# An attention layer's output projection: products per batch, or Strassen's seven products over pairs of batches

## The chip, the cores and the metric

One core of a Trainium2 chip runs the kernel. The time is device microseconds of one execution; the number given for a kernel is the median of its runs. Lower is better.

## What is computed

Multi-query attention with a residual, for 64 batches of 128 tokens, width 512, 16 heads of 64, one key and value head, all in float32:

```
xn = layernorm(x, g_in)
q = xn @ Wq                      # 512 -> 1024, 16 heads
k, v = xn @ Wkv                  # one head of 64 each, plus a null key and value
sim = q k^T + attn_bias          # causal and key mask set to a large negative
out = softmax(sim) @ v           # 128 x 1024 per batch
return x + layernorm(out @ Wo, g_out)     # Wo: 1024 -> 512
```

## The kernel before

The order of each engine's work is the program's order: a manual schedule, no reordering. `step(n)` runs for n = -6 to 62 and does one stage each for several batches: exponentials, block transpose and its DMAs for batch n+1, scores for n+2, values for n, output product and residual for n-1, and the input's norm, keys and query products some batches ahead. Tiles rotate in pools, so a write to a reused buffer waits for its last reader. [...]

- Query products (`product`, L408): groups of four batches; for each of four column parts f, seven products in Strassen's form with 256 output columns and two contraction chunks. `keep` (L419, ScalarE) copies an intermediate out of PSUM (kp1, ku2, ku3), `q_out` (L426 ScalarE, L429 VectorE) writes a quarter of qT, adding such a copy. Products 4 and 3 of part f come a step later. The token sums they need are GpSimd's (`token_sum`, L390), the weight sums VectorE's (`weight_sums`).
- Scores (`scores`, L474 and L485): first the upper 64 queries against all 128 keys, then the lower 64 against 64 keys. For each half VectorE adds the scores to the prepared bias rows S (L495) and takes the row maximum (L496). `bias_add` (L445) and `null_copy` on GpSimd prepare S; there are two S buffers.
- `exps` (L505): eight exponentials per half on ScalarE, then `rinv` (L522, VectorE) and `scale` (L526, GpSimd).
- `blocks_T` (L541): VectorE transposes S in 32x32 blocks into sb; `blocks_move` (L561) issues 14 DMAs on SP that carry the blocks to their places in aTb. One sb and one aTb buffer.
- `values` (L610): eight matmul calls into two `ps_w` banks (po), first with 64 rows, then with 128; ScalarE evacuates both into oT (L618).
- `out_mm` (L630): oT times Wo, eight chunks of 512 columns into one `ps_w` bank py. `out_stats` (L637 to L644): VectorE takes statistics of py and writes y = (py - mean) * g_out; GpSimd makes rstd. `residual`: ScalarE scales y by rstd (L658), GpSimd adds x (L659); `store` sends it.
- `norm_stats`/`norm_apply` (L231 to L249), `tokens_T` (L268), `k_T`/`kv_mm` into one bank pk (L298, L332) and their copies by VectorE (L310 to L337) prepare later batches.

In a float32 matmul call the profile shows two passes.

## Time and profile before

| | |
|---|---|
| median of 3 runs | 1196.62 us (1195.54 to 1200.66) |
| profiled execution | 1194.94 us; its span 1193.1 us |
| granted TensorE clock | 0.991 |
| output product L630 | 453.6 us busy in 1024 passes |
| query products L408 | 1680 passes of 256 columns |
| steady window 300 to 600 us | TensorE busy 300.0, VectorE 189.3, ScalarE 172.7, GpSimd 171.4 |

Busy time of overlapping instructions is counted once per engine; a row's mean is the time of one instruction from start to end, and pipelined instructions overlap by some of it. The last column of a row is the idle time just ahead of it on its engine, with what ended it.

### The profile page before, as it was taken

To read this page: it belongs to the slowest core of one execution; us is meant where nothing else is said; L and a number is where in the kernel's file an instruction comes from. 1 tells how busy PE (TensorE), PEld (TensorE's weight loads), DVE (VectorE), ACT (ScalarE), POOL (GpSimd) and SP (SyncE) were. 2 spreads that over 40 slices of the span, in tenths; PEclk is the share of its full clock that TensorE was granted. 3 is DMA by queue.
4 is the path that set the end of the run, shared out by engine and by line. 5 is a ranking of instruction groups with operands and counts; after the bars stand their busy time and mean duration, and the time that the engine had idled before them with its cause. 6 is when DMAs were issued, how large, how long until landed. Compare 5 with 4: busy or idle time off the path is not lost.

```text
span 1193.1 us, 22640 instructions
## 1 busy us (share of the span) xinstructions
PE 1151.9 (97%) x7588; PEld 747.9 (63%) x7588; DVE 716.2 (60%) x1449; ACT 652.1 (55%) x2625; POOL 654.4 (55%) x524
## 2 busy tenths in 40 slices
PE   6888999999999999999999999999999999999887
PEld 4465666666666666666666666666666666666433
DVE  6565566566666656656665665666566565545552
ACT  2254555565565556556555655655665565555551
POOL 5453755556475555647555465746546574654641
PEclk9998999999999999999999999999999999999999
DMA  6314334343533434343343434334353433422221
GB/s 185 111 39 127 96 124 122 119 122 90 143 95 122 121 112 130 90 136 103 122 115 116 131 91 133 105 123 111 111 140 90 130 99 106 102 74 71 70 81 45
DMA packets 107844, 129.79 MB, mean 109 GB/s; under 512 B 29264, under 2 KB 72528, under 8 KB 105936
## 3 DMA queue, kind: packets, MB, share of 16 engines
q1 hardware_dynamic: 106912, 127.29, 37.2%
q8 instruction: 61, 1.00, 0.4%
q10 hardware_dynamic: 816, 1.05, 0.2%
q14 instruction: 55, 0.45, 0.1%
HBM read 54.86 MB, written 31.46 MB: 72 GB/s over the span
## 4 chain that ended last, share of the span: by engine, by line
PE 86%; SPq 4%; DVE 2%; DMA 1%; issue 1%; ACT 0%; POOL 0%; DVEq 0%; ACTq 0%
PE py L630 35%; PE pa L408 17%; PE pc L408 8%; PE po L610 8%; PE ps L474 5%; PE pk L298 5%; PE pw L408 4%; SPq L561 4%; PE ps L485 3%; DMA aTb<-sb 1%; DVE sb L541 1%; PE pk L332 1%; DMA res<-in_x_dram 0%; DVE s L495 0%; PE paL L582 0%
## 5 line engine op out<-in xcount | busy, mean ns | idle before, releaser
L630 PE MATMUL py<-wo,oT 128*128 128x512 f32 x1024 | 453.6, 596 | 1.9 <-ACT oT L618 1.9
L445 POOL TENSOR_TENSOR s<-biasp,mneg 128x1536 f32<-128x1536 f32 x64 | 220.8, 3451 | 292.6 <-DVE sb L541 193.6
L505 ACT ACTIVATE s<-s,nmax 128x129 f32<-128x129 f32 (+1 forms) x1024 | 368.8, 365 | 0.0
L630 PEld LDWEIGHTS py<-wo,oT 128*128 128x128 f32 x1024 | 195.3, 191 | 223.9 <-issue 217.0
L526 POOL TENSOR_TENSOR s<-s,rinv 128x1024 f32<-128x1024 f32 (+1 forms) x128 | 188.4, 1479 | 15.5 <-DVE rinv L522 11.3
L505 ACT ACTIVATION_READ_ACCUMULATOR s<-s,nmax 128x1 f32 x1024 | 194.1, 190 | 0.0
L618 ACT ACTIVATE oT<-po,nv 128x512 f32<-128x512 f32 x128 | 81.3, 685 | 185.3 <-PE po L610 185.1
L495 DVE TENSOR_TENSOR s<-ps,s 128x1024 f32<-128x1024 f32 (+1 forms) x128 | 121.7, 951 | 68.9 <-PE ps L474 66.0
L659 POOL TENSOR_TENSOR y<-y,res 128x512 f32<-128x512 f32 x63 | 80.3, 1274 | 151.0 <-ACT y L658 151.0
L522 DVE RECIPROCAL rinv<-rsum 128x8 f32<-128x8 f32 x128 | 25.9, 203 | 209.7 <-ACT s L505 208.2
L408 PE MATMUL pa<-xS,wS 128*128 128x256 f32 x480 | 130.6, 395 | 0.7 <-ACT ku L419 0.7
L496 DVE TENSOR_REDUCE nmax<-s 128x8 f32<-128x1032 f32 (+1 forms) x128 | 123.1, 962 | 4.4
L610 PE MATMUL po<-aTb,vs 128*64 128x256 f32 (+1 forms) x768 | 109.8, 393 | 1.8 <-DVE aTb L589 1.7
L541 DVE STREAM_TRANSPOSE sb<-s 128x1536 f32<-128x1536 f32 x62 | 109.7, 1769 | 0.1
L419 ACT COPY ku<-pa 128x256 f32<-128x256 f32 x120 | 44.7, 373 | 116.1 <-PE pa L408 114.5
L408 PEld LDWEIGHTS pa<-xS,wS 128*128 128x128 f32 x480 | 83.0, 191 | 30.3 <-issue 20.0
L249 ACT ACTIVATE x<-x,nmr,rstd 128x512 f32<-128x512 f32 x60 | 48.7, 813 | 86.3 <-DVE nmr L248 85.9
L429 DVE TENSOR_TENSOR qT<-pw,kp 128x256 f32<-128x256 f32 x60 | 25.5, 425 | 98.5 <-ACT kp L419 98.5
L474 PEld LDWEIGHTS ps<-kT,qT 64*128 64x128 f32 x1024 | 62.5, 188 | 22.5 <-issue 21.8
L474 PE MATMUL ps<-kT,qT 64*128 64x128 f32 x1024 | 74.9, 286 | 0.0
L426 ACT COPY qT<-pa 128x256 f32<-128x256 f32 x60 | 22.4, 372 | 92.1 <-PE pa L408 92.1
L637 DVE BATCH_NORM_STATS2 sto<-py 128x6 f32<-128x512 f32 x64 | 44.8, 699 | 44.6 <-PE py L630 44.5
(90 smaller groups left out, 1547.4 us busy)
## 6 DMA issues: line engine op xcount, KB each, us to landing
aTb<-sb SPq DMA_DIRECT2D x372, 64.0 KB
x<-in_x_dram SPq DMA_DIRECT2D x64, 256.0 KB
res<-in_x_dram SPq DMA_DIRECT2D x64, 256.0 KB
out_dram<-y SPq DMA_DIRECT2D x64, 256.0 KB
aTb<-sb SPq DMA_DIRECT2D x496, 32.0 KB
xd<-xb SPq DMA_DIRECT2D x14, 1024.0 KB
xT<-xd SPq DMA_DIRECT2D x56, 256.0 KB
wo<-in_L_cond_Wo_dram SPq DMA_DIRECT2D x1, 2048.0 KB
```

Source lines behind the costliest of these rows:

```text
L408: nc.tensor.matmul(prod[tag], w[:, kc, f * P : (f + 1) * P], t[:, :, kc, :], start=(start and kc == 0), stop=(kc == HK - 1), skip_group_ch ...
L445: nc.gpsimd.tensor_tensor(S[b][:, :, 1 : ROW - 1], biasp, mneg[g][:, t].unsqueeze(1).broadcast_to([P, R8, NL + N]), ALU.add,)
L474: nc.tensor.matmul(pv[:, r, f, :], qT[g][rows, f, t, 1].rearrange("p u i -> p (u i)"), kT[b][rows, :], start=True, stop=True,)
L495: nc.vector.tensor_tensor(sv, pv, sv, ALU.add)
L496: nc.vector.tensor_reduce(nmax[b][:, hf], S[b][:, :, WITH_NULL[hf]], AX.X, ALU.max, negate=True)
L505: nc.scalar.activation(row, row, AF.Exp, bias=nmax[b][:, hf, k : k + 1], accum_out=rsum[b][:, hf, k : k + 1],)
L526: nc.gpsimd.tensor_tensor(sv, sv, rinvs.pop((b, hf)).unsqueeze(2).broadcast_to([P, R8, sv.shape[2]]), ALU.mult,)
L541: nc.vector.transpose(sb.rearrange("p j e q -> p e j q"), S[b][:, :, 1 : ROW - 1].rearrange("p e (j k) -> p e j k", k=Q),)
L610: nc.tensor.matmul(po[u][r * DH : (r + 1) * DH, half], vals, aTb[rows, slots, r * NF : (r + 1) * NF], start=True, stop=True,)
L618: nc.scalar.activation(oT[b][:, u * NF : (u + 1) * NF, :].rearrange("p f (s q) -> p s f q", q=Q), po[u].rearrange("p h i f q -> p (h i) f q"),
L630: nc.tensor.matmul(py, oT[b][:, c, :], wo[:, c, :], start=(c == 0), stop=(c == NC - 1))
L659: nc.gpsimd.tensor_tensor(y, y, res.pop(b), ALU.add)
```

## The change

Batches 1 to 60 are taken in 30 pairs (p, p+1), p odd; 0, 61, 62 and 63 stay as they were. A pair's two 128x1024 by 1024x512 products become seven products of half size, with 256 output columns and four contraction chunks each. GpSimd makes four sums of oT halves per pair, in place, and four sums of Wo halves once. Products 1 and 2 are issued in the even step n = p+1, products 5, 6, 7 and 3 in n = p+2, product 4 in n = p+3. Two new one-bank PSUM buffers X and Y (`ps_y`) hold the running sums; `ps_s` goes from two score buffers to one. `out_keep` and `out_part` move the results, and write y in SBUF in halves. `pair_norm` writes the normed rows into bank Y, `pair_residual` multiplies by g_out and adds x on VectorE. Both batches are stored together, and the residual is loaded one step later.

Also moved: lower scores before upper, each added as soon as it is there, the upper ones after the values; the block transpose right after the first add; the exponentials in parts between the other ScalarE work; `norm_apply` after them; query product 2 (in odd steps to the front); token sums 1 and 2 to the end of the step before; a weight sum to GpSimd, in place of its input.

```diff
-    ps_s = ctx.enter_context(tc.tile_pool(name="ps_s", bufs=2, space=PSUM))
+    ps_s = ctx.enter_context(tc.tile_pool(name="ps_s", bufs=1, space=PSUM))
     ps_q = ctx.enter_context(tc.tile_pool(name="ps_q", bufs=1, space=PSUM))
+    ps_y = ctx.enter_context(tc.tile_pool(name="ps_y", bufs=1, space=PSUM))
...
     def loads_late(n):
-        if 0 <= n:
+        if 1 <= n and not plain(n - 1):
+            load_res(n - 1)
+        if 0 <= n and plain(n):
             load_res(n)
...
-        nc.vector.tensor_tensor(s3, a11, a21, ALU.subtract)
...
+    def weight_sum_3():
+        nc.gpsimd.tensor_tensor(s3, a11, a21, ALU.subtract)
...
-    KEYS = UK, LK
-    WITH_NULL = slice(1 + NL, ROW), slice(0, 1 + NL)
+    KEYS = LK, UK
+    WITH_NULL = slice(0, 1 + NL), slice(1 + NL, ROW)
...
+    def scores_add(b, hf):
+        sv = S[b][:, :, KEYS[hf]].rearrange("p (r f) j -> p r f j", r=2)
+        nc.vector.tensor_tensor(sv, pss.pop((b, hf)), sv, ALU.add)
...
-    def exps(b, hf):
-        if hf == 0:
+    def exps(b, hf, lo=0, hi=R8):
+        if hf == 0 and lo == 0:
             rsum[b] = small.tile([P, 2, R8], FP, tag="rsum", name=f"rsum_{b}")
-        for k in range(R8):
+        for k in range(lo, hi):
             row = S[b][:, k, WITH_NULL[hf]]
...
+    def paired(p):
+        return 1 <= p <= P_LAST and p % 2 == 1
+    def plain(b):
+        return not (paired(b) or paired(b - 1))
+    def out_weight_sum(k):
+        p, m = ((e12, e11), (e22, wT[:, 0]), (e22, e12), (e21, wT[:, 1]))[k]
+        nc.gpsimd.tensor_tensor(wT[:, k], p, m, ALU.subtract)
+    def out_sums(p):
+        yS[p] = bp.tile([P, HC, N], FP, tag="yS", name=f"yS_{p}", bufs=1)
+        h11, h12 = oT[p][:, lo_c], oT[p][:, hi_c]
+        h21, h22 = oT[p + 1][:, lo_c], oT[p + 1][:, hi_c]
+        nc.gpsimd.tensor_tensor(yS[p], h21, h22, ALU.add)
+        nc.gpsimd.tensor_tensor(h21, h11, h21, ALU.subtract)
+        nc.gpsimd.tensor_tensor(h11, yS[p], h11, ALU.subtract)
+        nc.gpsimd.tensor_tensor(h12, h12, h11, ALU.subtract)
+    def out_product(p, k, pool, tag, start=True):
+        key = "y" + tag
+        if start:
+            prod[key] = pool.tile([P, HE], FP, tag=tag, name=f"py{tag}_{p}_{k}")
+        a, b = oT[p], oT[p + 1] if p + 1 in oT else None
+        h, w = {
+            1: lambda: (a[:, lo_c], e11),
+            2: lambda: (a[:, hi_c], e21),
+            3: lambda: (a[:, hi_c], e22),
+            4: lambda: (b[:, hi_c], wT[:, 3]),
+            5: lambda: (yS[p], wT[:, 0]),
+            6: lambda: (a[:, lo_c], wT[:, 1]),
+            7: lambda: (b[:, lo_c], wT[:, 2]),
+        }[k]()
+        for c in range(HC):
+            nc.tensor.matmul(
+                prod[key],
+                h[:, c, :],
+                w[:, c, :],
+                start=(start and c == 0),
+                stop=(c == HC - 1),
+                skip_group_check=not start,
+            )
+    def out_keep(tag, name, slot):
+        kept[name] = bp.tile([P, HE], FP, tag=f"k{slot}", name=f"k{name}", bufs=1)
+        if name == "yu2":
+            nc.vector.tensor_copy(kept[name], prod["y" + tag])
+        else:
+            nc.scalar.copy(kept[name], prod["y" + tag])
+    def out_part(b, e, tag, name=None):
+        if b not in ys:
+            ys[b] = hp.tile([P, DIM], FP, tag="y", name=f"y_{b}", bufs=3)
+        o = ys[b][:, lo_e if e == 0 else hi_e]
+        if name is None:
+            nc.scalar.copy(o, prod["y" + tag])
+        else:
+            nc.vector.tensor_tensor(o, prod["y" + tag], kept.pop(name), ALU.add)
+    yn = {}
+    def pair_stats(b):
+        st = small.tile([P, 6], FP, tag="st", name=f"sto_{b}")
+        nc.vector.bn_stats(st, ys[b])
+        mv = small.tile([P, 2], FP, tag="mvo", name=f"mvo_{b}")
+        nc.vector.bn_aggr(mv, st)
+        rstd = small.tile([P, 1], FP, tag="rstdo", name=f"rstdo_{b}")
+        nc.vector.tensor_scalar(rstd, mv[:, 1:2], EPS, None, ALU.add)
+        nc.gpsimd.tensor_tensor(rstd, rstd, nhalf, ALU.pow)
+        yn[b] = mv, rstd
+    def pair_norm(b):
+        mv, rstd = yn.pop(b)
+        nmr = small.tile([P, 1], FP, tag="nmro", name=f"nmro_{b}")
+        nc.vector.tensor_scalar(nmr, mv[:, 0:1], rstd, -1.0, ALU.mult, ALU.mult)
+        yn[b] = ps_y.tile([P, DIM], FP, tag="Y", name=f"yn_{b}")
+        nc.scalar.activation(yn[b], ys[b], AF.Identity, bias=nmr, scale=rstd)
+    def pair_residual(b):
+        z = yn.pop(b)
+        nc.vector.tensor_tensor(z, z, gob, ALU.mult)
+        nc.vector.tensor_tensor(ys[b], z, res.pop(b), ALU.add)
...
-        y = hp.tile([P, DIM], FP, tag="y", name=f"y_{b}")
+        y = hp.tile([P, DIM], FP, tag="y", name=f"y_{b}", bufs=3)
...
         fast, last = q and qg > 0, 0 < last_g < NG
+        p12, p4, p5673 = n - 1, n - 3, n - 2
+        first, third, second = paired(p12), paired(p4), paired(p5673)
+        one = ok(n - 1) and plain(n - 1)
         fill = n <= 0
+        soft = ok(n + 1) and not fill
         if part == 0 and ok(qg + 1, NG) and n + 6 >= 0:
             load_mask(qg + 1)
-        if ok(n + 2) and n >= 0:
+        if second:
+            out_sums(p5673)
+        elif ok(n + 2) and n >= 0:
             bias_add(n + 2)
+            null_copy(n + 2)
         for m in mns:
             norm_stats(m)
-        if fast and f == 0:
-            token_sum(qg, 1)
-            if fill:
-                for k in range(2, 5):
-                    token_sum(qg, k)
+        if fast and f == 0 and fill:
+            for k in range(1, 5):
+                token_sum(qg, k)
+            if n == -2:
+                weight_sum_3()
         if n == -4:
             bias_add(0)
             bias_add(1)
-        if ok(n + 2):
+        if ok(n + 2) and n < 0:
             null_copy(n + 2)
+        if third:
+            out_product(p4, 4, ps_y, "X", start=False)
+        if one:
+            out_mm(n - 1)
+            out_stats(n - 1)
+        if fast:
+            if f == 0:
+                q_tile(qg)
+            if n % 2:
+                product(qg, f, 2, ps_w, "w")
+        if last:
+            product(last_g, last_f, 4, ps_q, "a", start=False)
+        if soft:
+            exps(n + 1, 0, 0, 4)
+        if third:
+            out_part(p4 + 1, 0, "X")
+        if last:
+            q_out(last_g, HC + last_f, lo_t, "a")
+            product(last_g, last_f, 3, ps_q, "c", start=False)
+            q_out(last_g, last_f, hi_t, "c", "u2")
+        if third:
+            pair_stats(p4 + 1)
         if 2 * GB <= mb < B:
             tokens_T(mb)
             if (mb + 1) % GB == 0:
                 tokens_out(mb // GB)
         if (n + 7) % GB == 0 and 2 <= (n + 7) // GB < NG:
             tokens_in((n + 7) // GB)
-        if ok(n + 1) and not fill:
-            exps_half(n + 1, 0)
-            exps_half(n + 1, 1)
-        if ok(n - 1):
-            out_mm(n - 1)
-            out_stats(n - 1)
-        if fast and f == 0 and not fill:
-            for k in range(2, 5):
-                token_sum(qg, k)
-        if last:
-            product(last_g, last_f, 4, ps_q, "a", start=False)
-            q_out(last_g, HC + last_f, lo_t, "a")
-            product(last_g, last_f, 3, ps_q, "c", start=False)
-            q_out(last_g, last_f, hi_t, "c", "u2")
+        if soft:
+            exps(n + 1, 0, 4)
+            rinv(n + 1, 0)
+            scale(n + 1, 0)
+        if third:
+            pair_norm(p4)
+            pair_residual(p4)
+        if second and ok(n + 2):
+            bias_add(n + 2)
+            null_copy(n + 2)
         if ok(n + 1) and fill:
             exps_half(n + 1, 0)
-        for m in mns:
-            norm_apply(m)
         if part == 3 and ok(n + 3):
             nulls_move((n + 3) // GB, slice(0, GB - 1))
         if part == 0 and ok(n + 2):
             nulls_move((n + 2) // GB, slice(GB - 1, GB))
+        if first:
+            out_product(p12, 1, ps_y, "X")
+        if fast and n % 2 == 0:
+            product(qg, f, 2, ps_w, "w")
+        elif q and not fast:
+            q_plain(qg, 2 * f)
+        if soft:
+            exps(n + 1, 1, 0, 2)
+        if second:
+            out_product(p5673, 5, ps_y, "Y")
+            out_keep("Y", "yp5", "u3")
+        if first:
+            out_keep("X", "yp1", "p1")
+        if third:
+            pair_norm(p4 + 1)
+            pair_residual(p4 + 1)
+        if soft:
+            exps(n + 1, 1, 2, 4)
+        if first:
+            out_product(p12, 2, ps_w, "w")
+            out_part(p12, 0, "w", "yp1")
+        if soft and not second:
+            exps(n + 1, 1, 4)
+            rinv(n + 1, 1)
+            scale(n + 1, 1)
         if fast:
-            if f == 0:
-                q_tile(qg)
-            product(qg, f, 2, ps_w, "w")
             product(qg, f, 1, ps_q, "a")
             keep("a", "p1")
             q_out(qg, f, lo_t, "w", "p1")
+        if second:
+            out_product(p5673, 6, ps_y, "X", start=False)
+            out_keep("X", "yu2", "yu2")
+        if soft and second:
+            exps(n + 1, 1, 4)
+            rinv(n + 1, 1)
+            scale(n + 1, 1)
+        for m in mns:
+            norm_apply(m)
+        if fast and f == 0 and not fill:
+            for k in range(3, 5):
+                token_sum(qg, k)
+        if fast:
             product(qg, f, 5, ps_q, "c")
-        elif q:
-            q_plain(qg, 2 * f)
+        if f == GB - 1 and n > 0 and ok(qg + 1, NG):
+            token_sum(qg + 1, 1)
+        if second:
+            out_product(p5673, 7, ps_y, "X", start=False)
+            out_part(p5673 + 1, 1, "X", "yp5")
+            out_product(p5673, 3, ps_y, "Y", start=False)
+            if part == 3 and q:
+                mask_neg(qg)
+            out_part(p5673, 1, "Y", "yu2")
         if ok(n + 1) and fill:
             exps(n + 1, 1)
-        if ok(n - 1) and q:
+        if one:
             residual(n - 1)
         if ok(n + 2):
             scores(n + 2, 0)
-            if not q and n + 1 < B - 2:
-                blocks_T(n + 1)
+            scores_add(n + 2, 0)
             if ok(n + 1) and fill:
                 rinv(n + 1, 1)
                 scale(n + 1, 1)
-            scores(n + 2, 1)
+        if soft and n + 1 < B - 2:
+            blocks_T(n + 1)
+        if ok(n + 2):
+            scores_max(n + 2, 0)
         if n == B - 2:
             attn_T_pe(n)
         if ok(n):
             values(n)
-        if ok(n - 1) and not q:
-            residual(n - 1)
+        elif fast:
+            product(qg, f, 6, ps_q, "a", start=False)
+            keep("a", "u2")
         if n + 1 in sbs:
             blocks_move(n + 1)
-        if fast:
+        if ok(n + 2):
+            scores(n + 2, 1)
+            scores_add(n + 2, 1)
+            scores_max(n + 2, 1)
+        if fast and ok(n):
             product(qg, f, 6, ps_q, "a", start=False)
             keep("a", "u2")
-        elif q:
+        elif q and not fast:
             q_plain(qg, 2 * f + 1)
+        if f == GB - 1 and n > 0 and ok(qg + 1, NG):
+            token_sum(qg + 1, 2)
         if n + 10 < 2 * GB:
             norm_T(n + 10)
         if ok(mkv) and mkv >= GB - 1:
             pk = ps_w.tile([P, KVN + N], FP, tag="w", name=f"pk_{mkv}")
             k_T(mk, pk[:, KVN:])
             kv_mm(mkv, pk[:, 0:KVN])
-        if ok(n - 1):
+        if one:
             store(n - 1)
+        if third:
...
-        if ok(n + 1) and q and not fill:
-            blocks_T(n + 1)
-            blocks_move(n + 1)
+        if fast:
+            product(qg, f, 7, ps_q, "a", start=False)
+            keep("a", "u3")
+            q_out(qg, HC + f, hi_t, "c", "u3")
+        if second:
+            pair_stats(p5673)
         if ok(mkv) and mkv >= GB - 1:
             kT_out(mk, pk[:, KVN:])
             kv_out(mkv, pk[:, 0:KVN])
-        if fast:
-            product(qg, f, 7, ps_q, "a", start=False)
-            keep("a", "u3")
         if ok(mk) and not ok(mkv):
             kT_out(mk, k_T(mk))
-        if fast:
-            q_out(qg, HC + f, hi_t, "c", "u3")
         if ok(n + 1) and fill:
             blocks_T(n + 1)
             blocks_move(n + 1)
+        if 0 <= n < 4:
+            out_weight_sum(n)
         if n == -4:
             for m in range(GB - 1):
                 kv_out(m, kv_mm(m))
                 if m:
                     kT_out(m - 1, k_T(m - 1))
-        if part == 3 and 0 < qg < NG:
+        if part == 3 and 0 < qg < NG and not second:
             mask_neg(qg)
```

More of the change, by code (lines that the diff above doesn't have):

```diff
@@ L342 @@
     lo_t, hi_t = slice(0, HT), slice(HT, TOK)
-    wS = const.tile([P, 4, HK, HF], FP, name="wS")
+    wS = const.tile([P, 3, HK, HF], FP, name="wS")
     a11, a12 = wq[:, lo_k, 0:HF], wq[:, hi_k, 0:HF]
     a21, a22 = wq[:, lo_k, HF:], wq[:, hi_k, HF:]
-    s1, s2, s3, s4 = (wS[:, i] for i in range(4))
+    s1, s2, s4 = (wS[:, i] for i in range(3))
+    s3 = a21
     xS, prod, kept = {}, {}, {}
@@ L427, in q_out @@
         else:
-            k = kept[name].rearrange("p (t h i) -> p t h i", t=2, h=2)
+            k = kept.pop(name).rearrange("p (t h i) -> p t h i", t=2, h=2)
             nc.vector.tensor_tensor(o, p, k, ALU.add)
@@ L457, in null_copy @@
         )
-    KEYS = UK, LK
-    WITH_NULL = slice(1 + NL, ROW), slice(0, 1 + NL)
+    KEYS = LK, UK
+    WITH_NULL = slice(0, 1 + NL), slice(1 + NL, ROW)
     def scores(b, hf):
         g, t = divmod(b, GB)
-        nk = N if hf == 0 else NL
+        nk = N if hf == 1 else NL
         ps = ps_s.tile([P, 2, NF, N], FP, tag="s", name=f"ps_{b}_{hf}")
@@ L470, in scores @@
         for f in range(NF):
-            if hf == 0:
+            if hf == 1:
                 for r in range(2):
@@ L491, in scores, with scores_max @@
                         )
+        pss[b, hf] = pv
+    pss = {}
+    def scores_add(b, hf):
+        sv = S[b][:, :, KEYS[hf]].rearrange("p (r f) j -> p r f j", r=2)
+        nc.vector.tensor_tensor(sv, pss.pop((b, hf)), sv, ALU.add)
+    def scores_max(b, hf):
         if hf == 0:
             nmax[b] = small.tile([P, 2, R8], FP, tag="nmax", name=f"nmax_{b}")
-        sv = S[b][:, :, KEYS[hf]].rearrange("p (r f) j -> p r f j", r=2)
-        nc.vector.tensor_tensor(sv, pv, sv, ALU.add)
         nc.vector.tensor_reduce(
@@ L498, in scores @@
         )
-    def exps(b, hf):
-        if hf == 0:
+    def exps(b, hf, lo=0, hi=R8):
+        if hf == 0 and lo == 0:
             rsum[b] = small.tile([P, 2, R8], FP, tag="rsum", name=f"rsum_{b}")
-        for k in range(R8):
+        for k in range(lo, hi):
             row = S[b][:, k, WITH_NULL[hf]]
@@ L633, in out_mm @@
         ys[b] = py
+    HE = DIM // 2
+    P_LAST = B - 5
+    lo_e, hi_e = slice(0, HE), slice(HE, DIM)
+    lo_c, hi_c = slice(0, HC), slice(HC, NC)
+    wT = const.tile([P, 4, HC, HE], FP, name="wT")
+    e11, e12 = wo[:, lo_c, lo_e], wo[:, lo_c, hi_e]
+    e21, e22 = wo[:, hi_c, lo_e], wo[:, hi_c, hi_e]
+    yS = {}
+    def paired(p):
[5 more added lines that the diff above has]
+        nc.gpsimd.tensor_tensor(wT[:, k], p, m, ALU.subtract)
@@ L801, in step @@
             kv_mm(mkv, pk[:, 0:KVN])
-        if ok(n - 1):
+        if one:
             store(n - 1)
+        if third:
+            store(p4)
+            store(p4 + 1)
         loads_late(n)
-        if ok(n + 1) and q and not fill:
-            blocks_T(n + 1)
-            blocks_move(n + 1)
+        if fast:
[4 more added lines that the diff above has]
+            pair_stats(p5673)
         if ok(mkv) and mkv >= GB - 1:
```

## The prediction

> **What bounds the kernel now.** I read the page first: its engine shares, then the chain that ended last.
>
> ```profile
> span 1193.1 us, 22640 instructions
> ...
> PE 1151.9 (97%) x7588; PEld 747.9 (63%) x7588; DVE 716.2 (60%) x1449; ACT 652.1 (55%) x2625; POOL 654.4 (55%) x524
> ...
> PE 86%; SPq 4%; DVE 2%; DMA 1%; issue 1%; ACT 0%; POOL 0%; DVEq 0%; ACTq 0%
> ```
>
> TensorE is the bound, the other three have four tenths of their time free, and the chain runs over TensorE except at start and end. How a steady step is made up is in the chain in order of time, of the stretch 600 to 640 us (start, length, what):
>
> ```profile
> 608.42 6.87 PE py L630 x16
> 615.29 0.86 PE pa L408 x4
> 616.15 0.86 PE pc L408 x4
> 617.01 0.86 PE pw L408 x4
> 617.88 0.86 PE pa L408 x4
> 618.74 0.86 PE pc L408 x4
> 619.60 1.09 PE ps L474 x16
> 620.70 0.62 PE ps L485 x32
> 621.32 1.53 PE po L610 x16
> 622.85 1.06 PE pa L408 x4
> 623.91 0.11 PE pk L332
> 624.02 0.98 PE pk L298 x8
> 625.01 0.86 PE pa L408 x4
> 625.87 6.87 PE py L630 x16
> ```
>
> No piece of another engine stands between: a step is 625.87-608.42 = 17.45 us of TensorE, two are 34.90. The chain after 1090 us is different: no query products are left, and a step of some 13.3 us is a block transpose, 14 DMA issues and a landing.
>
> **What the product itself saves.** Sixteen 512-column passes take 6.87 us, so a pair costs 13.74. In the query products, which have the Strassen form already, four 256-column passes take 0.86: 0.215 each, the weight load (0.19) hidden. A pair's seven products are 7 x 8 = 56 such passes, 12.04 us. Saved: 1.70 us per pair, 30 pairs (batches 1 to 60): 51 us if nothing else moves. Everything below asks what of it is left.
>
> **TensorE's new order.** The upper scores (1.09) now come after the values (po), so the array goes 64 rows (lower scores, first po half), 128 rows (second po half), 64 rows, 128 rows. In the old step a change of row tiling shows in its price:
>
> ```profile
> 619.53 0.97 PEld L474 LDWEIGHTS ps<-kT,qT 64*128 64x128 f32 x16 [0.33 <-issue]
> 621.77 0.63 PEld L610 LDWEIGHTS po<-aTb,vs 128*64 128x64 f32 x8 [0.39 <-issue]
> ```
>
> and pa after po is 1.06 instead of 0.86. So the old step has three changes at about 0.2, the new one four. [...] I take 0.4.
>
> **The even step, by queues.** Step n even does products 4 of the pair before (p=n-3) and 1 and 2 of the new one (p=n-1); odd steps do 5, 6, 7, 3. Take t=0 at the end of the last query product (7) of the odd step. TensorE: product 4 to 1.72, query 4 and 3 to 3.44, product 1 to 5.16, query 2 to 6.02, product 2 to 7.74, query 1 and 5 to 9.46, lower scores (0.2 of change + 0.62) to about 10.3, then po. The second po tile reuses the bank of query product 2. That bank is read by VectorE's q_out, which adds ScalarE's copy kp1; and kp1 now stands on ScalarE behind all exponentials and both pair_norm. In the old step it had only norm_apply ahead of it and came while TensorE worked on. So does the copy come in time? VectorE, all in its order, with these rows:
>
> ```profile
> L249 ACT ACTIVATE x<-x,nmr,rstd 128x512 f32<-128x512 f32 x60 | 48.7, 813 | 86.3 <-DVE nmr L248 85.9
> L618 ACT ACTIVATE oT<-po,nv 128x512 f32<-128x512 f32 x128 | 81.3, 685 | 185.3 <-PE po L610 185.1
> ```
>
> - 3.48: q_out after query 3 (0.34), statistics of the pair's second half from SBUF (the x statistics row L231: 0.72+0.22+0.07), token transpose L268 (0.63), reciprocal (0.13), nmr (0.20): 5.8. VectorE was busy until then with q_out, a pair_stats, the three copies of pk and one norm_stats (2.9 us from 0.45).
> - pair_norm of the first batch on ScalarE: an Identity with pointer scale and bias that writes PSUM. No row shows it. Nearest is L249, 0.81, same form into SBUF; from below L618, 0.685. [...] I take 0.78, with the waits 6.6.
> - pair_residual: two VectorE adds and multiplies of 512 out of PSUM, the first also into it. The row of L495 with 512 elements (PSUM, SBUF into SBUF) is 0.68; bounds 0.6 and 0.8. With two handovers of 0.04: 8.1.
> - nmr of the second batch, and its pair_norm, which must wait because both use the one bank Y: 8.25 to 9.0.
> - six remaining exponentials at 0.388 (trace spacing of L505): 11.3; kp1 0.37; q_out 0.42 with handovers: 12.15.
>
> TensorE is ready for that po tile at about 10.5 (the first two passes of the other tile need only product 2's reader, done at 10.8). So it stands 1.6 us in every even step. Queued behind it on TensorE: the rest of po (1.3), upper scores 1.09, query 6 1.06, pk 1.09, query 7 0.86, 5.4 in all; ScalarE's oT, VectorE's second score add and the next step's exponentials wait for those. Even step 12.15+5.4 = 17.55.
>
> **The odd step.** Five query pieces 4.30, four products 6.88, scores, po, upper scores, query 6, pk, query 7 with four changes: 17.65 if nothing waits. I checked each wait in that frame (u=0 at its start): GpSimd's four out_sums (4 x 1.27, row L390) begin after oT at about u=-2.7, so product 5 (u=2.6) and 6 (u=5.2) have their operands at -1.5 and 1.1. VectorE's copy yu2 between product 6 and 7 is done at 7.3, wanted at 7.74. The lower score add ends at 12.75, upper scores (one score buffer instead of two) want it at 13.6. These are covers of 0.4 to 4 us; each gone costs its excess one to one.
> In the even step the score add (12.9) is covered by po (13.45).
>
> **Edits that I cost at nothing.** GpSimd loses two residual adds per pair (2 x 1.27) and gains four sums: +2.5 us in 35, of which it had 15 idle; its worst place is rstd of the second half behind bias_add (3.45+0.21), ready at 7.2, used at 8.0. The token sums moved ahead fill its gaps. VectorE gains 3 x 0.42 + 0.4 + 4 x 0.68 + 0.4 less 2 x 0.74: +3.3 per pair, outside the chain above in its own gaps. ScalarE: three copies of 0.37. SP: 14 block issues at about 0.64 (9.0) now go before the stores; the store of the pair's first batch lands (2.1 to 2.6) near u=9.4, when its y buffer is written again at 9.5; being 1 us late would still be covered. The residual load has a step less to arrive, at 9.2 against 9.75 wanted. The aTb blocks land about 3 us ahead of po_odd and 2 ahead of po_even. mask_neg, weight_sum_3 and the four out_weight_sum (2.5 each on GpSimd, in steps 0 to 3) lie in the start, where GpSimd is half idle: between -3 and +3, taken 0, because the earlier block transpose helps by as much. Tail: GpSimd's and ScalarE's work comes before the transposes of batches 59 and 61, so by the same rows four block rounds take about 45 us instead of 41 (1108.5 to 1149.4 in the chain), with the first one some 3 earlier: +2.
>
> **Sum.** Pair 17.55+17.65 = 35.20 against 34.90: +0.30. In 28 pairs that have query work: +8; tail +2. The profiled execution took 1194.94 (span 1193.1 and 1.8 around it): 1205. The median of the runs is 1.7 above it: **1207**. [...]
>
> **Rivals.**
> - *Chain shorter (not slower).* The place is the same handover of kp1 in the even step. From 3.44 it is 8.7 us long; each 0.1 is worth 2.8 us. At both low ends (pair_norm 0.69 twice, PSUM operations 0.6 each) it is 0.5 shorter; with a tiling change that costs nothing the pair is 34.3: 28 x -0.6 + 2: about 1182. It decides from a chain below 8.3. [...] Against it: L249 is the same form. Chance 0.17.
> - *Full gain.* kp1 isn't late at all: pair 33.2+0.4, 28 x -1.3: 1162. It would need three of the steps above to overlap that are in one queue or on one bank. Chance 0.06.
> - *A second wait.* High ends (0.1 each on four operations, changes 0.4): pair +1.1 to +1.2, 1230; or the residual's landing, the y store or yu2 lose their 0.1 to 0.6 of cover, 0.5 to 1 us per pair: 1220 to 1235. For it: three covers under 0.6. Chance 0.32.
> - The forecast, 1197 to 1216: 0.45.
> The transfers can't hide the change: TensorE's work does fall.
>
> **Chances.** 0.5% (6 us) is about what a measurement of this kernel can tell from no change: 1190.6 to 1202.6. Faster: 0.06 and most of 0.17, 0.22. Same: the lower part of my forecast and the rest, 0.18. Slower 0.60. Range 1185 to 1232: below lies the full gain and some of the first rival, above the ends of the second wait. As cases of both signs hold weight: the forecast's own range is 1197 to 1216.
>
> **What would show it.** Right: TensorE busy near 94%, po waiting on DVE q_out or ACT kp about 1.6 us some 28 times, odd steps without a gap, products of about 1.72, two steps in 35.2. Wrong: no such wait (gain comes), a VectorE multiply in PSUM or a pair_norm far from 0.68 and 0.78, or TensorE waiting on Pool yS/oT, on aTb DMAs, or on the copy yu2 in the odd step.

## The result, and the profile after

The changed kernel takes 1307.42 us (median of 4 runs, 1303.23 to 1317.32) against 1197.19 us for the kernel before beside it: ratio 1.093, 95% interval 1.086 to 1.100. The forecast was 1207 with a range to 1232; the sign was right and the size wrong by 100 us.

Lines below are numbered as in the changed kernel: query products L421, values L630, token sums L403, `bias_add` L458, output products L700, `out_part` L723, the pair's rstd L734, `pair_norm` L740 and L744, `pair_residual` L748 and L749, block transfers L581, token transfers L294. In experiments with the query copy moved, the last four move down by nine (L744 is L753 there). First the page: span, engine shares, granted clock in 40 slices.

```profile
span 1301.3 us, 24550 instructions
...
PE 1170.1 (90%) x8308; PEld 914.0 (70%) x8308; DVE 812.5 (62%) x1688; ACT 688.9 (53%) x2715; POOL 744.4 (57%) x589
...
PEclk9988998998989999898989999898998989999898
```

TensorE's busy time went up by 18 us although the products are some 49 us shorter (30 pairs at 1.64 us, as e12 below shows), and its clock is below 0.9 in 14 of the 40 slices. Both say one thing: matmuls that run at half clock are busy for longer (a product of eight passes takes 3.78 us there and 1.89 at full clock, both in this trace). The chain of this page breaks off after two pieces, so I took the start of the values of every batch from the timeline, and the distance from one batch to the next but one, which is a pair of steps. Before it is 34.90 us. After, nine of the 26 pairs from batch 5 to batch 57 take 35.0 to 35.4, most of them 35.31 (the forecast was 35.20); five take 36.9 to 37.0; and twelve, which come every four steps, take 38.3 to 42.8. One line for each kernel, of a good pair; the columns are busy time of PE, PEld, DVE, ACT and POOL, granted clock, DMA share, GB/s:

```profile
603.74:638.64 34.90, 34.90 (x247) 23.06 (x239) 22.27 (x47) 20.27 (x82) 22.61 (x19) 1.00 0.41 107
```

```profile
606.67:641.99 35.32, 33.95 (x260) 27.75 (x259) 24.01 (x52) 21.05 (x83) 19.27 (x16) 1.00 0.35 108
```

So the pair that the forecast worked out exists, to 0.1 us, with 1.4 us of TensorE waiting at the place it named. It is the other pairs that cost. The list of waits of the changed kernel (waiting engine and line, releaser: total us, times, longest us) names them:

```profile
POOL xS L403 <- DMA aTb<-sb: 114.8, 12, 11.5
...
PE po L630 <- DVE y L723: 64.0, 29, 5.8
...
DVE nmro L740 <- POOL rstdo L734: 33.7, 21, 2.2
```

The first row is GpSimd's token sum. It reads only xT; the wait is put down to a block transfer of the same SP queue, so that it is the tokens that are late is a reading, which e2 below tests. How it reaches TensorE is in the timeline of one such pair (start, length, engine, line, operation, and in brackets the idle time ahead with its releaser):

```profile
575.03 1.95 SPq L294 DMA_DIRECT2D xT<-xd  x4
...
586.68 1.27 POOL L403 TENSOR_TENSOR xS<-xT 128x512 f32<-128x512 f32 x1 [10.14 <-DMA aTb<-sb]
...
589.77 3.45 POOL L458 TENSOR_TENSOR s<-biasp,mneg 128x1536 f32<-128x1536 f32 x1
...
593.95 0.55 POOL L734 TENSOR_TENSOR rstdo<-rstdo,nhalf 128x1 f32<-128x1 f32 x1
...
594.84 0.78 ACT L744 ACTIVATE yn<-y,nmro,rstdo 128x512 f32<-128x512 f32 x1 [2.50 <-DVE nmro L740]
...
597.00 0.42 DVE L723 TENSOR_TENSOR y<-pyw,kyp 128x256 f32<-128x256 f32 x1
...
597.47 1.12 PE L630 MATMUL po<-aTb,vs 64*64 64x256 f32 x4 [3.82 <-DVE y L723]
```

The tokens are issued at 575.0, and the sum cannot start until 586.7. Behind the waiting sums on GpSimd stand the pair's rstd, a `bias_add` of 3.45 and the second rstd; behind that rstd the second norm; behind the norm, on ScalarE and VectorE, the readers that free the values' bank. TensorE stands 3.8 us. Then the clock, in stretches of the same pair (the column ahead of the last two is the granted clock):

```profile
594.00:596.80 2.80, 0.00 (x0) 0.00 (x0) 1.32 (x3) 1.96 (x8) 1.51 (x2) 1.00 0.53 142
...
598.50:600.20 1.70, 1.50 (x8) 0.61 (x8) 0.90 (x3) 0.81 (x1) 1.70 (x2) 0.50 0.08 25
...
601.90:603.60 1.70, 1.70 (x16) 1.63 (x16) 0.68 (x2) 0.65 (x1) 1.70 (x2) 0.50 0.10 26
603.60:606.00 2.40, 2.40 (x18) 2.10 (x15) 2.10 (x2) 0.37 (x1) 2.24 (x3) 0.96 0.26 65
```

The clock records of this trace have it at 0.50 from 596.95 to 603.78. Of these 6.8 us 6.3 lie behind the wait, and by the 3.78 us against 1.89 of a product, work that takes 6.3 us at half clock takes about 3.2 us less at full clock, an estimate. The start has the same pair of losses, with the fourth weight sum, which I had taken at nothing:

```profile
160.46 2.34 POOL L673 TENSOR_TENSOR wT<-wo,wT 128x1024 f32<-128x1024 f32 x1
...
162.85 3.78 PE L700 MATMUL pyX<-wT,oT 128*128 128x256 f32 x8 [4.97 <-POOL wT L673]
```

The product waits 4.97 us and then takes 3.78 instead of 1.89.

### The profile page after: what moved, and what is told of

It is laid out like the page before. It is cut to its first block, busy times and chain, and to the rows that moved or that the text cites. A ratio compares the mean times of both kernels' runs of the same rounds, so it can differ in the third digit from the quotient of the medians.

```text
span 1301.3 us, 24550 instructions
## 1 busy us (share of the span) xinstructions
PE 1170.1 (90%) x8308; PEld 914.0 (70%) x8308; DVE 812.5 (62%) x1688; ACT 688.9 (53%) x2715; POOL 744.4 (57%) x589
## 5 line engine op out<-in xcount | busy, mean ns | idle before, releaser
L525 ACT ACTIVATE s<-s,nmax 128x65 f32<-128x65 f32 (+1 forms) x1024 | 371.6, 367 | 4.8 <-DVE nmax L516 4.4
L546 POOL TENSOR_TENSOR s<-s,rinv 128x512 f32<-128x512 f32 (+1 forms) x128 | 189.0, 1477 | 135.7 <-DVE rinv L542 135.6
L458 POOL TENSOR_TENSOR s<-biasp,mneg 128x1536 f32<-128x1536 f32 x64 | 220.8, 3451 | 13.4 <-DVE sb L561 13.0
L630 PE MATMUL po<-aTb,vs 128*64 128x256 f32 (+1 forms) x768 | 128.4, 452 | 58.3 <-DVE y L723 54.8
L700 PE MATMUL pyX<-wT,oT 128*128 128x256 f32 x720 | 172.7, 383 | 7.2 <-POOL wT L673 5.0
L700 PEld LDWEIGHTS pyX<-wT,oT 128*128 128x128 f32 x720 | 137.1, 191 | 28.3 <-POOL wT L673 5.4
L511 DVE TENSOR_TENSOR s<-ps,s 128x512 f32<-128x512 f32 (+1 forms) x128 | 121.7, 951 | 36.6 <-PE ps L487 25.5
L421 PE MATMUL pa<-xS,wq 128*128 128x256 f32 x480 | 123.8, 380 | 2.4 <-ACT ku L432 1.4
L516 DVE TENSOR_REDUCE nmax<-s 128x8 f32<-128x520 f32 (+1 forms) x128 | 120.4, 941 | 6.0 <-POOL s L467 3.7
L630 PEld LDWEIGHTS po<-aTb,vs 128*64 128x64 f32 (+1 forms) x768 | 49.5, 153 | 106.2 <-DVE y L723 58.5
L734 POOL TENSOR_TENSOR rstdo<-rstdo,nhalf 128x1 f32<-128x1 f32 x60 | 32.9, 549 | 150.8 <-DVE rstdo L733 150.8
L403 POOL TENSOR_TENSOR xS<-xT 128x512 f32<-128x512 f32 x30 | 38.2, 1272 | 130.0 <-DMA aTb<-sb 114.8
L744 ACT ACTIVATE yn<-y,nmro,rstdo 128x512 f32<-128x512 f32 x60 | 46.9, 781 | 96.2 <-DVE nmro L740 96.2
L421 PEld LDWEIGHTS pa<-xS,wq 128*128 128x128 f32 x480 | 87.1, 190 | 13.1 <-ACT ku L432 2.4
L442 DVE TENSOR_TENSOR qT<-pc,ku 128x256 f32<-128x256 f32 x120 | 50.9, 424 | 62.1 <-ACT ku L432 40.5
L748 DVE TENSOR_TENSOR yn<-yn,gob 128x512 f32<-128x512 f32 x60 | 42.0, 700 | 52.7 <-ACT yn L744 52.7
```

What stands on the lines that cost most here:

```text
L421: nc.tensor.matmul(prod[tag], w[:, kc, f * P : (f + 1) * P], t[:, :, kc, :], start=(start and kc == 0), stop=(kc == HK - 1), skip_group_ch ...
L442: nc.vector.tensor_tensor(o, p, k, ALU.add)
L458: nc.gpsimd.tensor_tensor(S[b][:, :, 1 : ROW - 1], biasp, mneg[g][:, t].unsqueeze(1).broadcast_to([P, R8, NL + N]), ALU.add,)
L511: nc.vector.tensor_tensor(sv, pss.pop((b, hf)), sv, ALU.add)
L516: nc.vector.tensor_reduce(nmax[b][:, hf], S[b][:, :, WITH_NULL[hf]], AX.X, ALU.max, negate=True)
L525: nc.scalar.activation(row, row, AF.Exp, bias=nmax[b][:, hf, k : k + 1], accum_out=rsum[b][:, hf, k : k + 1],)
```

## The experiments

*Theory* after the result: the forecast's chain holds, and the loss comes from covers that I costed at nothing (order on SP, token sums and weight sums on GpSimd), made larger by the half clock behind stalls. *Rivals*: the new order on TensorE is itself too long; or the stall of the even step alone does it, by the clock.

All in us; beside the experiments the kernel before took 1194.9 to 1196.6. Three columns split the profiled span: start to the values of batch 5, to those of batch 57, to the end. The last one is how long the granted clock was 0.50 between batches 5 and 57.

| kernel | median | ratio (95%) | start | 5 to 57 | end | half clock |
|---|---|---|---|---|---|---|
| before | 1195 to 1197 | 1 | 184.4 | 908.3 | 100.4 | 0 |
| changed | 1307.42 | 1.093 (1.086 to 1.100) | 194.7 | 990.3 | 116.3 | 102.4 |
| e1_sums_back | 1294.53 | 1.082 (1.078 to 1.086) | 190.2 | 975.4 | 116.8 | 88.7 |
| e2_xt_early | 1267.97 | 1.061 (1.057 to 1.065) | 190.1 | 952.5 | 115.9 | 47.8 |
| e3_no_pairs | 1416.58 | 1.186 (1.183 to 1.187) | 196.6 | 1109.4 | 108.1 | 177.5 |
| e5_kp1 | 1269.09 | 1.060 (1.057 to 1.064) | 196.4 | 952.5 | 119.4 | 20.5 |
| e6_all | 1257.81 | 1.052 (1.049 to 1.055) | 187.6 | 953.4 | 116.3 | 61.4 |
| e7_sp_order | 1253.23 | 1.048 (1.046 to 1.051) | 195.0 | 939.5 | 114.6 | 41.0 |
| e8_best | 1215.65 | 1.017 (1.014 to 1.020) | 189.2 | 907.7 | 115.9 | 10.2 |
| e9_best_tail | 1213.96 | 1.015 (1.011 to 1.019) | 188.0 | 910.7 | 119.0 | 20.5 |
| e10_tokens_after | 1188.03 | 0.993 (0.991 to 0.996) | 188.5 | 884.0 | 114.0 | 0 |
| e11_tail | 1199.03 | 1.002 (1.000 to 1.003) | 187.9 | 883.9 | 124.3 | 0 |
| e12_last_step | 1181.18 | 0.987 (0.985 to 0.989) | 184.5 | 883.8 | 107.0 | 0 |
| e13_sp_only | 1248.54 | 1.045 (1.042 to 1.048) | 195.4 | 942.2 | 116.9 | 54.6 |

**e1_sums_back** puts the token sums 1 and 2 of a group behind the pair's first rstd on GpSimd.

```diff
-        if f == GB - 1 and n > 0 and ok(qg + 1, NG):
-            token_sum(qg + 1, 1)
...
-        if f == GB - 1 and n > 0 and ok(qg + 1, NG):
-            token_sum(qg + 1, 2)
...
         if third:
             pair_stats(p4 + 1)
+        if fast and f == 0 and not fill:
+            for k in range(1, 3):
+                token_sum(qg, k)
```

> The changed kernel with token sums 1 and 2 issued on GpSimd in the even step, after the rstd of the pair's second half, and not at the end of the odd step. Theory A (every fourth step GpSimd stands about 10 us at token sum 1, for the token transfer, and the pair's rstd behind it on its queue comes 4 us late, so that po starts late): the wait goes, all pairs take about 35.3 us, 26 x 2.8 = 70 us less, about 1235. Rival B (the order of ScalarE, VectorE and bank Y alone makes those pairs long): within 20 us of 1307.

Only 13 us came back, which by the number alone is the rival's range. The trace decides otherwise: the sums block nothing any more, and the next cover of the same step is gone instead. The residual is late, with 29.7 us of waits (4.9 in the changed kernel); in one pair VectorE stands 3.04 us for it, and TensorE behind that 3.54.

```profile
DVE y L749 <- DMA res<-in_x_dram: 29.7, 18, 4.0
```

**e2_xt_early** issues the token transfers a step earlier, ahead of the block transfers of the even step.

```diff
-        if (n + 7) % GB == 0 and 2 <= (n + 7) // GB < NG:
-            tokens_in((n + 7) // GB)
...
+        if (n + 8) % GB == 0 and 2 <= (n + 8) // GB < NG:
+            tokens_in((n + 8) // GB)
         if n + 1 in sbs:
             blocks_move(n + 1)
```

> The changed kernel with the four token transfers issued on SP one step earlier, ahead of the 14 block transfers of the even step; GpSimd's order unchanged. Theory A: the token sums find their data, same as when they are moved: about 1235, the idle time of the token sum from 130 us to under 20. Rival B: within 20 us of 1307. A third reading, that it is the sums' own 2.5 us on GpSimd and not the transfer: no gain here, a gain only when they are moved.

40 us came back of the 72 that the theory gave. The sums wait for no long transfer any more, which shows that the late tokens held them; they now wait for an earlier query product, the last reader of their buffer. And the stores are late, which go behind those issues:

```profile
POOL xS L403 <- PE pa L421: 63.4, 14, 7.0
...
DVE y L723 <- DMA out_dram<-y: 59.6, 14, 6.5
```

**e3_no_pairs** is e2 with no batch paired; the new order stays.

```diff
-    P_LAST = B - 5
+    P_LAST = -1
```

> The one before this with no batch paired: every output product is the old one of eight 512-column chunks, normed and stored per batch as before, while the new order of scores, transposes, exponentials and query products stays, and one score buffer. Tells what the reordering costs without the pairs. Theory A: little, 17.5 us per step, 1195 to 1210. Rival: the reordering and the single score bank cost as much as the pairs' stalls: above 1225.

It could not tell what it was made for. In the new order the 6.87 us product stands at the front of the step, and twelve of ScalarE's sixteen exponentials are queued behind a copy that waits for it, 60 times:

```profile
ACT qT L439 <- PE pa L421: 373.7, 60, 6.8
```

A step takes 21.3 us. The order fits only the short products; what the reordering costs by itself is read from e12 below instead.

**e5_kp1** takes the stall out of the even step alone: query products 2 and 1 go ahead of output product 1, and the copy kp1 with its reader ahead of the pair's norms (output product 2 also goes ahead of the second norm, and VectorE's second reciprocal behind the lower scores).

```diff
+        early = fast and soft and first
...
+        if early:
+            product(qg, f, 2, ps_w, "w")
+            product(qg, f, 1, ps_q, "a")
         if soft:
             exps(n + 1, 0, 4)
...
+        if early:
+            keep("a", "p1")
+            if third:
+                pair_nmr(p4)
+            q_out(qg, f, lo_t, "w", "p1")
         if third:
             pair_norm(p4)
             pair_residual(p4)
```

> The changed kernel with the early kp1 alone, SP's queue as it was. Theory A2: where the transfers are late, ScalarE still stands at pair_norm for the late rstd and y comes late, so only the other half of the pairs gains 1.4 us: about 1307-14x1.4 = 1287, 1275 to 1295. Rival (kp1 behind the exponentials is the cause of all): 1220 to 1240.

Good pairs fell from 35.31 to 34.0; the pairs with late transfers stayed at 38 to 41, and with query product 2 early TensorE itself stands for tokens in some of them, up to 3.1 us. **e6_all** is e5 with e2 and the weight sums in steps 0 and 1:

```diff
-        if 0 <= n < 4:
-            out_weight_sum(n)
+        if 0 <= n < 2:
+            out_weight_sum(2 * n)
+            out_weight_sum(2 * n + 1)
```

> Token transfers early; the four weight sums in steps 0 and 1, not 0 to 3; and in even steps query products 2 and 1 ahead of output products 1 and 2, with copy kp1 ahead of pair_norm and its VectorE reader before the first residual, output product 2's reader before the second. If the stall of 1.4 us in every even step is the wait for kp1 and for y behind the two residuals, as the prediction has it, po waits no more: pair about 33.7 to 34.0, start 7 us shorter, about 1307-72-7-28x1.4 = 1185, between 1170 and 1195. If VectorE or GpSimd as a whole is what limits the even step, the pair stays above 35 and the time above 1215.

Half of the pairs took 34.0, the rest 38 to 41.5, and the time was far above the 1170 to 1195 expected. The stores are the late ones (141.2 us of waits for them, 28 times); that a faster pair leaves them less cover is a reading, not tested alone. So the order on SP came next.

**e7_sp_order** changes SP alone: stores, residual and input loads, then the tokens, all ahead of the block transfers.

```diff
+        if soft and n + 1 < B - 2:
+            if third:
+                store(p4)
+                store(p4 + 1)
+            loads_late(n)
+        if (n + 8) % GB == 0 and 2 <= (n + 8) // GB < NG:
+            tokens_in((n + 8) // GB)
         if n + 1 in sbs:
             blocks_move(n + 1)
```

> The changed kernel with one edit on SP's queue: both stores, the loads of residual and x, and the token transfers stand ahead of the 14 block transfers of their step, not behind them. Theory A2 (three loads or stores that stand behind the block transfers land late, each hidden by the one before: token transfer, residual, y buffer): all three waits go (VectorE on the residual's DMA, on the store, GpSimd's token sum), pairs 35.3 to 35.6 throughout, about 1307-26x2.7 = 1235, and below the 1268 of the early token transfer alone. Rival: the block transfers, now later, become the late ones (po waits for aTb), no better than 1268.

54 us came back, and no waits for tokens, residuals or stores are left among the long ones. But the pairs are not 35.31 throughout, as expected: most are 35.31 or 36.88, two values 1.57 apart. **e8_best** adds the edit of e5 and the early weight sums:

> The same SP order with the weight sums in steps 0 and 1 and kp1 early in even steps. If the prediction's stall at kp1 is the rest: pairs 34.0 throughout, as in half of the pairs of the earlier combination, about 1194 + 28x(34.0-34.9) + 16 for the tail = 1185 (1178 to 1200). Rival: one of the waits stays and the clock halves with it, 1215 or more.

The rival came: every second pair is 34.0, but most of the others are 34.4 to 40.1. SP's timeline of one shows why: the 14 block issues behind the four token transfers took 15.9 us, where others take 9, and the values waited for a block (28.3 us, 16 times).

```profile
504.69 9.02 SPq L581 DMA_DIRECT2D aTb<-sb  x14
...
520.90 1.98 SPq L294 DMA_DIRECT2D xT<-xd  x4
523.02 15.89 SPq L581 DMA_DIRECT2D aTb<-sb  x14
```

**e9_best_tail** is e8 with `P_LAST = B - 9`, so that four more batches of the tail are not paired.

> The same with pairs only up to batch 56, so that the steps without query products are taken batch by batch. If the tail's 16 us come from the pairs' own chain in steps that have no query work to hide it: about 8 us less than with pairs up to 60. Rival: the tail is longer because of the order of scores, transposes and exponentials, and stays.

No gain that can be measured. At the change from pairs to plain batches, the two steps from batch 56 to batch 58 took 43.5 us where e8 took 31.2; the 9 us won behind them were given away there.

**e10_tokens_after** is e8 with the tokens behind the blocks instead of ahead of them.

```diff
-        if (n + 8) % GB == 0 and 2 <= (n + 8) // GB < NG:
-            tokens_in((n + 8) // GB)
         if n + 1 in sbs:
             blocks_move(n + 1)
+        if (n + 8) % GB == 0 and 2 <= (n + 8) // GB < NG:
+            tokens_in((n + 8) // GB)
```

> The version of e8 (stores, residual and input loads ahead of the block transfers on SP, weight sums in steps 0 and 1, query product 1 and its copy ahead of the pair's norm in even steps), with the four token transfers of a group issued right behind the 14 block transfers of the even step instead of ahead of them. In e8 the block transfers of such a step took up to 15.9 us on SP behind the token transfers, where others took 9, and the values waited up to 5.1 us for a block. Theory (order on SP decides what lands late): those pairs fall from 35 to 40 us to 34.0, the rest of e8's steady excess over 34.0 is 906.6 - 26 x 34.0 = 22.6 us, so about 1195, and no wait of the values for a block over 1 us in the steady part. Rival (1 MB of tokens is late wherever it is put, or the bandwidth itself is short): GpSimd's token sums wait for it again, 3 to 10 us, behind them the pair's norm, as in the changed kernel; 1220 or more.

Four issues moved past fourteen are worth some 28 us: all pairs are near 34.0, the clock is never at 0.50 from batch 5 to 57, and the kernel is faster than before. GpSimd's token sums do stand for these tokens, up to 6.7 us, as the rival expected, but no pair is longer for it. **e11_tail** moves the pair's norm and residual behind the values in the steps without query products:

```diff
+        late = third and not q
...
-        if third:
+        if third and not late:
             pair_norm(p4)
             pair_residual(p4)
...
+        if late:
+            for b in (p4, p4 + 1):
+                pair_norm(b)
+                pair_residual(b)
         if fast and ok(n):
```

> As e10, and in the steps without query products (58, 60, 62) the pair's norm and residual go behind the exponentials, the values and the second score add, stores and loads behind the block transfers. In e8 the last step lost 8.2 us because the pair's first norm on ScalarE waited for VectorE, which waited for the plain output product, with six exponentials queued behind it; the even tail steps took 16.6 us from block transpose to block transpose instead of 12.7. Theory (the tail's loss is the norm standing ahead of exponentials on the chain): 3.5 us in each of steps 58 and 60, 8 us in step 62, so 12 to 15 us below e10: about 1181 if e10 comes to 1195, faster than the kernel before (1195). Rival (the tail is bound by the 14 block issues and landings alone, and the norm only moves the wait): within 4 us of e10.

This theory fell: 11 us slower than e10. The last step shrank, but in steps 58 and 60 the wait only moved. The next product 5 uses the norm's bank Y, and everything on TensorE is queued behind it:

```profile
1097.68 3.75 PE L700 MATMUL pyY<-wT,yS 128*128 128x256 f32 x8 [9.32 <-DVE y L758]
```

**e12_last_step** is e10 with one move in step 62: `out_stats(61)` goes behind `pair_residual(60)`.

```diff
         if one:
             out_mm(n - 1)
-            out_stats(n - 1)
+            if not third:
+                out_stats(n - 1)
...
         if third:
             pair_residual(p4 + 1)
+            if one:
+                out_stats(n - 1)
```

> As e10, with one more move: in step 62 VectorE's statistics of the plain batch 61 go behind the norm and residual of batches 59 and 60. In e10 two steps to the values of batch 62 took 40.6 us where the kernel before takes 29.3: VectorE waits for the plain output product with the pair's scalars queued behind it, and ScalarE's six exponentials of the last batch wait behind the norm. e11 moved the norm instead, and in steps 58 and 60 the next product 5 then waited up to 9.3 us for bank Y, while step 62 shrank. Theory (a queue order in one step): 5 to 8 us below e10, about 1181. Rival (the end is bound by the output products and transposes in any case): within 2 us of e10's 1188.

As its theory expected: 1181.18, the best version, 1.3% below the kernel before. So the new order on TensorE is not too long in itself, and the first rival falls: batches 5 to 57 take 883.8 us against 908.3. A pair of it:

```profile
608.31:642.31 34.00, 33.50 (x264) 27.51 (x261) 24.32 (x53) 20.92 (x85) 20.92 (x17) 1.00 0.37 110
```

**e13_sp_only** is the changed kernel with SP's order as in e10 and nothing else: the forecast's own case, with its stall and its covers.

> The changed kernel with nothing but SP's order mended: stores, residual and input loads ahead of the block transfers, token transfers right behind them. The even step keeps the exponentials and norms ahead of the copy of query product 1, the start keeps its weight sums where they are. This is the forecast's own case: its even step of 17.55 and odd step of 17.65 us, with every cover it took for granted in place. Theory (the forecast failed at the covers, not at the chain): pairs 35.2 to 35.4 throughout, against 34.90; from batch 5 to 57 26 x 0.4 = +11, start +10, tail +14 as in the changed kernel: 1225 to 1235. Rival (the even step's stall of 1.4 us costs another 1.6 us of half clock whenever it comes, as in two pairs out of four of e7): mean pair 36.1, 1245 to 1253 as in e7.

The rival was right: 1248.5, pairs of 35.31 and of 36.88. Both kinds have the same stall; the timeline of two of them:

```profile
576.16 0.65 PE L630 MATMUL po<-aTb,vs 64*64 64x256 f32 x4 [0.69 <-DVE y L723]
577.48 0.65 PE L630 MATMUL po<-aTb,nv 64*64 64x256 f32 x4 [0.67 <-issue]
578.06 1.08 PE L630 MATMUL po<-aTb,vs 128*64 128x256 f32 x8
...
611.47 0.65 PE L630 MATMUL po<-aTb,vs 64*64 64x256 f32 x4 [0.70 <-DVE y L723]
612.79 0.65 PE L630 MATMUL po<-aTb,nv 64*64 64x256 f32 x4 [0.67 <-issue]
613.37 1.92 PE L630 MATMUL po<-aTb,vs 128*64 128x256 f32 x8
```

1.4 us of waiting is followed by full clock in the first case and by half clock in the second, which makes the pair 1.57 us longer. In stretches of 3.41 us, with TensorE's busy time behind the comma and the granted clock third from the end, the two cases are:

```profile
572.52:575.93 3.41, 2.95 (x43) 2.27 (x41) 2.43 (x6) 3.21 (x15) 1.08 (x2) 1.00 0.40 106
575.93:579.34 3.41, 2.51 (x20) 1.17 (x22) 1.94 (x6) 2.39 (x7) 2.36 (x2) 1.00 0.52 172
579.34:582.75 3.41, 3.41 (x32) 3.08 (x31) 3.38 (x4) 1.06 (x3) 3.33 (x4) 1.00 0.26 85
...
606.65:610.06 3.41, 3.41 (x17) 2.74 (x15) 1.91 (x4) 2.79 (x10) 2.23 (x4) 1.00 0.62 231
610.06:613.48 3.42, 2.06 (x43) 1.08 (x44) 2.67 (x7) 2.81 (x12) 1.19 (x1) 1.00 0.89 314
613.48:616.89 3.41, 3.41 (x24) 2.28 (x24) 2.35 (x2) 1.55 (x3) 1.52 (x2) 0.50 0.31 107
616.89:620.30 3.41, 3.41 (x23) 3.01 (x22) 2.45 (x2) 0.46 (x2) 3.17 (x4) 1.00 0.30 76
```

In the first case TensorE is idle for 0.46 and 0.90 us of the first two stretches, and the clock is 1.00 in all three. In the second it is idle for 1.36 us of the stretch from 610.06 to 613.48, and the next 3.41 us run at 0.50. What decides between the two is not shown by two cases. Between batches 5 and 57 of e13 the half clock comes to 54.6 us, 16 times 3.41, and 16 of the 26 pairs are the long ones.

## Why the prediction was wrong

The span grew by 108.2 us where the forecast had about 10: start +10.3, batches 5 to 57 +82.0, end +15.9. The step that failed is the one headed "Edits that I cost at nothing", with 48 of the 108; next come the half clock behind the stall of the even step, the tail and the start. By the forecast's own steps:

- **The product's saving** (1.70 per pair): right. In e12 a product takes 1.73 us from its start to the next start, seven take 12.1 instead of 13.74, 1.64 saved.

```profile
617.27 1.89 PE L700 MATMUL pyY<-wT,yS 128*128 128x256 f32 x8
619.00 1.03 PE L421 MATMUL pa<-xT,wq 128*128 128x256 f32 x4
```

- **The extra change of row tiling** (0.4 per pair): too high. No run shows the 0.4: lower scores to the end of query product 6 take 4.13 and 4.28 us in the two steps of e12, 4.22 in the kernel before, all from start to start. The net is about nothing.
- **The even step's chain**: the place and the wait are right, the size in part by luck. `pair_norm` takes 781 ns (0.78 taken), the multiply in PSUM 700 ns (0.68), and TensorE stands 1.4 us (1.6). But around the stall lower scores to query product 6 take 6.36 us where the odd step of the same pair takes 4.13: the stall costs 2.2. Beside the 1.4, the 64-row half of the values, 0.54 us long in the odd step, where its two tiles alternate, takes 0.65 and 0.58 when one tile comes after the other. That is 0.6 more than forecast, and it is hidden by the 0.4 for row tiling that did not come: 35.31 against 35.20. 26 pairs of 0.41 are 10.7 of the 82.0. The norm into PSUM takes 781 ns, against 814 for the same form into SBUF.

```profile
L744 ACT ACTIVATE yn<-y,nmro,rstdo 128x512 f32<-128x512 f32 x60 | 46.9, 781 | 96.2 <-DVE nmro L740 96.2
L258 ACT ACTIVATE x<-x,nmr,rstd 128x512 f32<-128x512 f32 x60 | 48.7, 814 | 34.5 <-DVE nmr L257 34.5
L748 DVE TENSOR_TENSOR yn<-yn,gob 128x512 f32<-128x512 f32 x60 | 42.0, 700 | 52.7 <-ACT yn L744 52.7
```

- **What a stall costs** was left out: I priced each wait one to one. In e13, where only the stall of the even step is left, batches 5 to 57 take 33.9 more than before: 10.7 by the chain, and the other 23.2 fit the half clock (16 pairs that are 1.57 longer make 25). e10 against e13 shows both ends: with the stall gone (and the start's sums) the middle is 58 us shorter, 2.24 per pair, of which the chain is 1.31.
- **"Edits that I cost at nothing"** is the step that failed. "The token sums moved ahead fill its gaps" looked at GpSimd's free time, not at when xT lands: the transfers were still issued where they had been, and the sums in front of the pair's rstd waited up to 11.5 us. The residual, the y store and the blocks, to which I gave 0.1 to 3 us of cover, each became the late one as soon as the one before it was mended (e1, e2, e6, e8). Together with their half clock they are 82.0 - 33.9 = 48 us: e13 differs from the changed kernel in nothing but the order on SP. About half of the 48 is clock, at most 24, since the middle has 102.4 us of half clock in one and 54.6 in the other.
- **The weight sums** in the start, "taken 0": a wait of 4.97 and 1.89 of half clock in one product, most of the start's +10.3. With the sums earlier the start is 188 to 189 in e8, e10 and e11, and 184.5 in e12, whose start is the same program; so some 4 us of it differ from one execution to the next. In e10 the clock is at half for 17.1 us of the start, in e12 for 10.2, which is 3.4 us of these 4.
- **The tail** (+2): +15.9. Step 62 alone is some 7 us of it (e10 against e12); e12 is still 6.6 above the kernel before there. What the remaining even steps cost isn't settled: e11 tried one cause and moved the wait.
- **The rivals**: the second wait was the right mechanism, but its price ("0.5 to 1 us per pair") was too low: almost every second pair is 3 to 7.5 us above 35.31. "Full gain" gave the pair 33.6 us with no late copy; e12, where the copy is early, takes 34.00, 0.5 to 0.7 of it one remaining wait of query product 5 for a bank.

## What to carry to other kernels

When work is moved ahead, move its inputs' transfers too, and write down for each queue, SP's included, what now stands in front of each transfer; the cover is the time from landing to need, not the free share of the engine. Cover that was worth tenths of a microsecond was none here: mended one at a time, the covers failed one after another, and only the order on SP as a whole (stores, loads, blocks, then tokens), together with the copy taken out of the chain, the earlier weight sums and one move in the last step, turned 9% slower into 1.3% faster. A TensorE stall is priced with the clock behind it: in e13 the same stall of 1.4 us was followed by half clock in 16 pairs of 26, which made each of them 1.57 us longer, and by full clock in the others.

## What the runs showed of the hardware

- Between batches 5 and 57 of the changed kernel the granted clock of TensorE was 0.50 for 102.4 us, in 15 stretches of 3.4 to 10.2 us, and in the 3.4 us ahead of each TensorE had stood idle for 1.3 to 3.3; in the kernel before, and in e10, e11 and e12, it never was there.
- A stall of 1.4 us, in two pieces 0.65 us apart, was followed by full clock in one pair of e13 and by 3.41 us at 0.50 in another; a stall of 3.8 us in the changed kernel was followed by 6.8 us at 0.50.
- In e8 the issue of 14 block transfers took 9.0 us on SP, and 15.9 behind four token transfers of 256 KB.
- The norm that writes PSUM with pointers for scale and bias takes 781 ns, between the two rows that bounded it (685 and 813).
